# A two-layer graph attention kernel: index loads on two queues, another order of loads and products between the first heads, another split of the last tile

## Chip, cores and metric

One core of one Trainium2 chip. The metric is the device time of one execution in microseconds (us). Engines: TensorE (PE; its weight loads are listed as PEld), VectorE (DVE), ScalarE (ACT), GpSimd (POOL) and SyncE (SP, which only issues DMAs here). ScalarE and GpSimd issue DMAs too. A difference of 0.2% is 1.2 us.

## The reference

A graph of 512 nodes and 16,896 edges (8,192 pairs, each in both directions, and a loop at each node), sorted by destination. Two graph attention layers, a residual sum and a layer norm:

```python
def gat_layer(x, W, a_s, a_d, b, edge_index, concat):
    n = x.shape[0]
    H, C = a_s.shape
    h = (x @ W).reshape(n, H, C)
    src, dst = (edge_index[0], edge_index[1])
    alpha_s = jnp.einsum('nhc,hc->nh', h, a_s)
    alpha_d = jnp.einsum('nhc,hc->nh', h, a_d)
    e = jax.nn.leaky_relu(alpha_s[src] + alpha_d[dst], NEG_SLOPE)
    m = jax.ops.segment_max(e, dst, num_segments=n)
    e = jnp.exp(e - m[dst])
    denom = jax.ops.segment_sum(e, dst, num_segments=n)
    alpha = e / (denom[dst] + EPS)
    msg = h[src] * alpha[:, :, None]
    out = jax.ops.segment_sum(msg, dst, num_segments=n)
    ...
h = gat_layer(x, W1, a_src1, a_dst1, b1, edge_list, concat=True)   # 8 heads of 768
h = jax.nn.elu(h)
out = gat_layer(h, W2, a_src2, a_dst2, b2, edge_list, concat=True) # 1 head of 768
...
x = _layernorm(x + out, axis=-1)
```

x is 512 x 768, W1 768 x 6144, W2 6144 x 768, all float32.

## The kernel before

The edges are never gathered. A matrix `cnt` of 512 x 512 counts the edges of each pair of nodes, and the attention of a head is a dense 512 x 512 matrix: scores from two vectors of logits, a mask where the count is 0, an exponential, a row sum. All large products are float32, and are done by schemes that need fewer multiplications than the plain product: seven products instead of eight on halves (functions with `P1` to `P7`), or fifteen instead of eighteen on a 2 by 3 by 3 partition (`by_thirds`, `P0` to `P14`). Their sums of operands are made on VectorE or by DMAs that add into their target (`add_up`, issued by GpSimd), and each product that leaves PSUM is added to its place.

The order on every engine is the order in which the program is written (`manual_schedule`). The kernel is written out by hand in this order:

- **Start.** The edge indices are loaded as integers into `idx_i` (66 partitions; lines 94 to 96), then x and the weights of head 0 (lines 237 to 270). TensorE does matmuls of zeros meanwhile (`keep_warm`, lines 280 to 285). `idx_i` is cast to float32 (L372), turned by TensorE into `psi` (L376), and x's first chunks are turned (`turn_x`, L316, copied to `xT` by ScalarE, L317). VectorE makes `fold`, `low` and `rel` from `psi` (L382 to L387), from them the one-hot matrices (L739 to L761), and TensorE counts with them (L787) between the products of head 0's projection (L649, L431).
- **Heads 0 and 1.** The projection of head 1 (by halves), head 0's attended sum (`near_first`, L1078), head 0's share of the second layer (`second` by halves into `h2`, L1261 to L1311), and the projection of head 2 (L1408 to L1436, by halves, products P1, P2, P6, P7, P4, P5, P3 with two row blocks each; evictions at L470 to L476). In these stages the scores of the next head are made (`score`, `scored`), and each of its four tiles is weighed, scaled and parted: `turn_out` scales it on ScalarE (L967), parts the halves of its words (L970) and has SP issue a transposing DMA (L972); `turn_in` (L975) joins them again into `PT`.
- **Heads 1 to 6.** For each: the attended sum (`mixed`, L1038, three rounds of 28 matmuls of 128 x 256; it ends with the exponential linear unit, L984 to L987, which writes `gT`), then the head's share of the second layer (`second_by_thirds`: 15 products of 8 matmuls, L505), and the projection of the head after the next (15 products too).
- **End.** Head 7, the second layer's attention, and the result tile by tile (L1544 to L1575): product, residual, `bn_stats`, mean and deviation, scaling, store.

Lines that the prediction's steps touch. In `turn_out`, the two operations on ScalarE and the DMA:

```python
nc.scalar.activation(q, q, AF.Copy, scale=rden)                                    # L967
nc.scalar.copy(apart..., q...)                                                     # L970
nc.sync.dma_start(parted[t].rearrange("p (j d) -> p j d", d=P), apart, transpose=True)  # L972
```

In `by_thirds`, each product has an accumulation chain, a target and a sign. A chain keeps one PSUM bank; the bank is taken from the pool `mm` (5 banks) when the chain is first used:

```python
STEPS = dict(P8=("a", (1, 2), 1.0), P13=("x", (1, 2), -1.0), ..., P2=("y", (0, 0), 1.0), P4=("x", (1, 0), 1.0), ...
```

The left sides of head h's share (`g_thirds`): P2's is a part of `gT` as it is (chunks 0 and 3, first half of the nodes); P13's is made by VectorE from two parts (L1200). Products in `by_dma` are copied out by ScalarE (L515) and added into `h2` by a DMA that GpSimd issues (L516); others are added by VectorE (L518).

`load_a` (L220) loads a head's two attention vectors, each broadcast to 128 partitions, on SP's queue. `load_second` (L199) loads the second layer's weights of a head: `load_pairs`, `load_first` and `load_rest` issue loads on SP (L147, L153, L161) and additions on GpSimd (L135). The logits of head 2 are made at L1432 (`logits`, L449) behind the evictions of the products 10 and 12 of its projection.

Of the kernel before, what the change touches and what calls it, by code (L numbers as in the profile page):

```python
# [8 lines left out]
F32 = mybir.dt.float32  # L9
# [30 lines left out]
def gat_pass(  # L40
# [17 lines left out]
    P = 128  # L58
# [33 lines left out]


    idx_i = ohp.tile([EH, 2, 2, P], I32, name="idx_i")
    for j, v in enumerate((dst, src)):
        nc.sync.dma_start(idx_i[:, j], v.rearrange("(r c p) -> c r p", p=P, c=EH))

    def load_x():
        t_ = hpool.tile([P, NT, D], F32, name="hs")
# [120 lines left out]
    def load_a(h, a_s, a_d):  # L220
        A[h] = []
        for name, a in (("a_s", a_s), ("a_d", a_d)):
            v = wpool.tile([P, D], F32, name=name)
            nc.sync.dma_start(v, row_bcast(a))
            A[h].append(v)
# [9 lines left out]
        return m[r * HK * P:(r + 1) * HK * P, cols].rearrange("(k p) d -> p k d", p=P)  # L235

    w1_0 = w1[:, :D]
    for t in range(2):
        nc.scalar.dma_start(x_sb[:, t, L], x[t * P:(t + 1) * P, L])
    for k in range(HK):  # L240
        nc.sync.dma_start(W1[0][0][:, k, L], block(w1_0, 0, L)[:, k])
    for t in range(2):
# [37 lines left out]
    def keep_warm(n, cols=512):  # L280
        for _ in range(n):
            nc.tensor.matmul(idle[:, :cols], zeros[:, :P], zeros[:, :cols], start=True, stop=True)

    keep_warm(8, P)
    keep_warm(5)
    nodes = ohp.tile([P, N], F16, name="nodes")
    nc.gpsimd.iota(nodes, pattern=[[1, N]], base=0, channel_multiplier=0,
                   allow_small_or_imprecise_dtypes=True)
# [34 lines left out]
    if general:  # L323
        nc.vector.tensor_copy(idx_f, idx_i)
        idx = ohp.tile([P, 2, EC], F32, name="idx")
        psi = tr.tile([P, 512], F32, name="tr")
        for j in range(2):
            for r in range(2):
                nc.tensor.transpose(psi[:, (2 * j + r) * EH:(2 * j + r + 1) * EH], idx_f[:, j, r, :],
                                    ident[:EH, :EH])  # L330
        nc.vector.tensor_copy(idx, psi[:, :2 * EC].rearrange("p (j c) -> p j c", j=2))
    else:

        B = 32
        blocks = []
        for c in range(EC):
            m = (c + 0.5) * P * N / E
            b = int(m // B)  # L340
            slack = 2 + 16 * (m / N * (1 - m / N)) ** 0.5
            lo, hi = b - (m - b * B < slack), b + ((b + 1) * B - m < slack)
            blocks.append(range(max(lo, 0), min(hi, N // B - 1) + 1))
        assert max(map(len, blocks)) <= 2


        QC = EC // NT
        QW = QC + QC % 2
        base = ohp.tile([P, EC], F32, name="base")
        two = ohp.tile([P, NT, QW], F16, name="two")  # L350
        rel = ohp.tile([P, NT, QW], F16, name="rel")
        weight = ohp.tile([P, 3, NT, QW], BF16, name="weight")

        def fill(values, put):
            lo = 0
            while lo < EC:
                hi = lo + 1
                while hi < EC and values[hi] == values[lo] and hi % QC:
                    hi += 1
                put(lo, hi, float(values[lo]))  # L360
                lo = hi

        fill([b[0] * B for b in blocks], lambda lo, hi, v: nc.gpsimd.memset(base[:, lo:hi], v))
        fill([len(b) > 1 for b in blocks],
             lambda lo, hi, v: nc.gpsimd.memset(two[:, lo // QC, lo % QC:lo % QC + hi - lo], v))
        if QW > QC:
            nc.gpsimd.memset(rel[:, :, QC:], -1.0)
            nc.gpsimd.memset(two[:, :, QC:], 0.0)
            nc.gpsimd.memset(weight[:, :, :, QC:], 0.0)
        offsets = ohp.tile([P, B, QW], F16, name="offsets")  # L370
        nc.scalar.copy(offsets, nodes[:, :B].unsqueeze(2).to_broadcast([P, B, QW]))
        nc.vector.tensor_copy(idx_f, idx_i)  # L372
        psi = tr.tile([P, 512], F32, name="tr")
        for j in range(2):
            for r in range(2):
                nc.tensor.transpose(psi[:, j * EC + r * EH:j * EC + (r + 1) * EH], idx_f[:, j, r, :], ident[:EH, :EH])  # L376
        turn_x(0, 0)
        turn_x(1, 0)
        quarters = lambda v: v.rearrange("p (q c) -> p q c", c=QC)
        fold = ohp.tile([P, EC], F32, name="fold")  # L380
        low = ohp.tile([P, EC], F32, name="low")
        nc.vector.tensor_scalar(fold, psi[:, EC:2 * EC], float(HN), -float(HN), op0=ALU.is_ge, op1=ALU.mult)  # L382
        nc.vector.tensor_tensor(low, psi[:, EC:2 * EC], fold, op=ALU.add)
        nc.vector.tensor_tensor(rel[:, :, :QC], quarters(psi[:, :EC]), quarters(base), op=ALU.subtract)
        nc.gpsimd.tensor_scalar(weight[:, 2, :, :QC], quarters(fold), -(DIGIT - 1) / HN, 1.0, op0=ALU.mult, op1=ALU.add)
        nc.vector.scalar_tensor_tensor(two, rel, float(B), two, op0=ALU.is_ge, op1=ALU.mult)
        nc.vector.scalar_tensor_tensor(rel, two, -float(B), rel, op0=ALU.mult, op1=ALU.add)  # L387
        nc.gpsimd.tensor_tensor(weight[:, 1], weight[:, 2], two, op=ALU.mult)
        nc.gpsimd.tensor_tensor(weight[:, 0], weight[:, 2], weight[:, 1], op=ALU.subtract)
# [94 lines left out]

    def by_thirds(dest, A_, B_, order, fresh, by_dma=()):

        bank, begun, free = {}, set(), list(passed)

        def out(o):
            return dest[:, 2 * o[0]:2 * o[0] + 2, o[1] * TH:(o[1] + 1) * TH]  # L490

        def step(p):
            chain, o, sign = STEPS[p]
            copied = fresh and o not in begun
            begun.add(o)

            def multiply(between=None):
                first = chain not in bank
                if first:
                    bank[chain] = mm.tile([P, 512], F32, name="mm")  # L500
                for i in range(2):
                    for k in range(2):
                        if between and i == k == 1:
                            between()
                        nc.tensor.matmul(bank[chain][:, i * TH:(i + 1) * TH], A_[p][:, k, i * P:(i + 1) * P], B_[p][:, k, :],  # L505
                                         start=first and i == k == 0, stop=k == 1, skip_group_check=True)

            def empty():
                ps = bank[chain].rearrange("p (i n) -> p i n", i=2)
                if copied:  # L510
                    nc.scalar.activation(out(o), ps, AF.Copy, scale=sign)  # L511
                elif p in by_dma:
                    free.append(free.pop(0))
                    part = free[-1].rearrange("p (i n) -> p i n", i=2)
                    nc.scalar.activation(part, ps, AF.Copy, scale=sign)  # L515
                    nc.gpsimd.dma_start(out(o), part, accum_op=ALU.add)  # L516
                else:
                    nc.vector.tensor_tensor(out(o), out(o), ps, op=ALU.add if sign > 0 else ALU.subtract)  # L518
            return multiply, empty

        return [step(p) for p in order]
# [5 lines left out]
                         True)  # L527

    def second_by_thirds(h, A_, B_):
        return by_thirds(h2, A_, B_, ("P13", "P2", "P8", "P4", "P12", "P9", "P6", "P0", "P1", "P14", "P10", "P5", "P11", "P7", "P3"),  # L530
                         False, ("P13", "P2", "P8", "P0", "P7", "P3") if h + 2 < H else ("P13", "P2", "P8", "P0"))

    def second(A_, B_):
# [701 lines left out]
    def out_by_dma(t):  # L1235
        turn_out(q[t], t, weigh(q[t], t, scale=False))
# [4 lines left out]
    for h in range(H - 1):  # L1241
# [14 lines left out]
        if h == 0:  # L1256
# [26 lines left out]
            for n in range(2, 7):  # L1283
# [16 lines left out]
                if 3 < n < 6:  # L1300
                    out_by_dma(n - 4)
                if n == 6:
                    out_by_dma(3)
                    B2, sums2, load_pairs, load_first, load_rest = load_second(1)
                    load_pairs()
                    load_first()
                    load_rest()
                    load_a(2, a_src1[2], a_dst1[2])
                e1()
                if n < 5:  # L1310
                    fold_count(n - 1)  # L1311
# [94 lines left out]
        elif not last:  # L1406
            B_, sums = right(W1[h + 2], "w2")
            pairs = projection(h + 2, XA, B_)  # L1408
            for n in range(14):
# [6 lines left out]
                if n == 1:  # L1416
                    AA, sums3 = left_sums(h + 1)
                pairs[n][1]()
                if n in (1, 2, 4):
                    turn_in((n + 2) // 2)  # L1420
                if n == 5:
# [122 lines left out]
    for t in range(NT):  # L1544
# [21 lines left out]
        ours = slice(0, D)  # L1566
        if t + 1 == NT:

            ours = L
            off = small.tile([P, 1], F32, name="off")  # L1570
            nc.vector.scalar_tensor_tensor(off, mv[:, 0:1], -1.0, rstd, op0=ALU.mult, op1=ALU.mult)
            nc.scalar.activation(y[:, t, R], y[:, t, R], AF.Identity, bias=off, scale=rstd)
            nc.scalar.dma_start(out[t * P:(t + 1) * P, R], y[:, t, R])
        nc.vector.tensor_scalar(y[:, t, ours], y[:, t, ours], mv[:, 0:1], rstd, op0=ALU.subtract, op1=ALU.mult)
        nc.sync.dma_start(out[t * P:(t + 1) * P, ours], y[:, t, ours])  # L1575
    return again
# [29 lines left out]
```

## Time and profile before

| | us |
|---|---|
| median of 3 runs | 621.42 (621.12 to 622.11) |
| the profiled execution | 622.47 |
| its span, first to last instruction | 620.7 |

| engine | busy us | share of the span | instructions |
|---|---|---|---|
| PE | 610.5 | 98% | 2770 |
| PEld | 483.2 | 78% | 2770 |
| DVE | 522.7 | 84% | 1137 |
| ACT | 335.1 | 54% | 608 |
| POOL | 150.5 | 24% | 188 |

The span runs from the first to the last instruction of the profiled execution; 1.8 us of its time lie outside. Times of rows are counted from the span's start. A row of the timeline has start, length, engine, line, operation, output and inputs, shape and how many instructions are merged; a float32 matmul is listed as two. Matmuls overlap in the pipeline, so the distance between starts, and not the length, tells their pace.

### The profile page before, as it was taken

The numbers are of one execution on the slowest core, as the hardware profiler recorded it, in microseconds if no ns is written. First come the engines' busy times: TensorE is split into PE (matmuls) and PEld (weight loads), VectorE is DVE, ScalarE is ACT, GpSimd is POOL, SyncE is SP. The second block draws the span as 40 slices with busy tenths as digits, with TensorE's granted clock in tenths as the row PEclk, the third lists the DMA queues.
The fourth block names the chain that finished last, engine by engine and source line by source line (L and its number), as shares of the span: only waits on it lengthen the run. The fifth ranks groups of instructions, "written<-read, shape, count | busy, mean of one in ns | idle before, by whom it ended". The sixth has DMA issues, their size and how long they took to land.

```text
span 620.7 us, 8565 instructions
## 1 busy us (share of the span) xinstructions
PE 610.5 (98%) x2770; PEld 483.2 (78%) x2770; DVE 522.7 (84%) x1137; ACT 335.1 (54%) x608; POOL 150.5 (24%) x188
## 2 busy tenths in 40 slices
PE   8999999999999999999999999999999999999995
PEld 5655685556888888888888888888888888885553
DVE  5999979887899879977897878977897878978785
ACT  4766867721858056841858046751758046754361
POOL 2210011032352332413343333313342313010000
PEclk9999999999999999999999999999999999999998
DMA  8994777899999999999999999999999995690032
GB/s 283 319 248 79 202 184 248 165 280 300 219 219 192 277 258 219 162 301 233 220 216 204 273 255 227 160 273 248 226 218 199 304 283 90 129 286 10 17 77 80
DMA packets 109969, 130.05 MB, mean 210 GB/s; under 512 B 41638, under 2 KB 90846, under 8 KB 109150
## 3 DMA queue, kind: packets, MB, share of 16 engines
q1 hardware_dynamic: 75918, 91.94, 49.3%
q0 software_dynamic: 33568, 36.90, 38.7%
q10 hardware_dynamic: 432, 0.59, 0.3%
q8 instruction: 24, 0.39, 0.3%
q14 instruction: 27, 0.22, 0.1%
HBM read 100.43 MB, written 2.90 MB: 166 GB/s over the span
## 4 chain that ended last, share of the span: by engine, by line
PE 89%; DMA 4%; DVE 4%; ACT 1%; issue 0%; SPq 0%; DVEq 0%; ACTq 0%
PE mm L505 46%; PE mm L1038 18%; PE mm L431 11%; PE mm L1078 6%; PE mm L1552 3%; PE held L431 2%; DMA a_d<-in_L_gnn_a_dst_dram 2%; DMA w1r<-in_L_gnn_W_dram 1%; PE tr L787 1%; PE held L649 1%; DVE scr L440 1%; DMA zr<-pS 1%; DMA idx_i<-in_src_dram 1%; PE mm L316 0%; ACT pS L970 0%
## 5 line engine op out<-in xcount | busy, mean ns | idle before, releaser
L511 ACT ACTIVATE hs<-mm 128x512 f32<-128x512 f32 x30 | 17.9, 596 | 84.9 <-PE mm L505 84.4
L1038 PE MATMUL mm<-PT,hs 128*128 128x256 f32 x216 | 52.5, 379 | 0.0
L518 DVE TENSOR_TENSOR hs<-hs,mm 128x512 f32<-128x512 f32 x45 | 30.9, 686 | 22.2 <-PE mm L505 21.4
L690 ACT ACTIVATE q<-q,nmax 128x512 f32<-128x512 f32 x32 | 23.1, 721 | 49.0 <-DVE nmax L686 48.9
L516 POOL DMA_DIRECT2D h<-pass x22 | 26.5, 1319 | 80.9 <-ACT pass L515 80.9
L1038 PEld LDWEIGHTS mm<-PT,hs 128*128 128x128 f32 x216 | 41.0, 190 | 5.8
L518 DVE TENSOR_TENSOR h<-h,mm 128x512 f32<-128x512 f32 x56 | 38.3, 684 | 6.3 <-PE mm L505 5.7
L975 ACT COPY PT<-zr 128x1024 uint16<-128x1024 uint16 x34 | 39.3, 1157 | 4.8 <-DMA zr<-pS 3.5
L505 PE MATMUL mm<-w2r,xT 128*128 128x256 f32 x160 | 37.8, 379 | 0.0
L505 PE MATMUL mm<-w2r,gT 128*128 128x256 f32 x160 | 37.0, 379 | 0.0
L1038 PE MATMUL mm<-pS,gS 128*128 128x256 f32 x144 | 37.0, 379 | 0.0
L135 POOL DMA_DIRECT2D w1t<-in_L_gnn_W_dram x18 | 27.7, 1577 | 26.3 <-DVE hs L1002 20.9
L505 PE MATMUL mm<-w1t,hs 128*128 128x256 f32 x144 | 34.1, 380 | 0.0
L505 PE MATMUL mm<-w1r,hs 128*128 128x256 f32 x144 | 34.1, 379 | 0.0
L505 PE MATMUL mm<-w1r,gS 128*128 128x256 f32 x144 | 34.0, 379 | 0.0
L505 PEld LDWEIGHTS mm<-w2r,gT 128*128 128x128 f32 x160 | 30.4, 190 | 4.1
L505 PEld LDWEIGHTS mm<-w2r,xT 128*128 128x128 f32 x160 | 30.4, 190 | 4.1
L1042 ACT COPY u<-mm 128x256 f32<-128x256 f32 x18 | 6.7, 372 | 43.9 <-PE mm L1038 43.9
L505 PEld LDWEIGHTS mm<-w1t,hs 128*128 128x128 f32 x144 | 27.3, 190 | 3.9 <-ACT absent L515 0.2
L1038 PEld LDWEIGHTS mm<-pS,gS 128*128 128x128 f32 x144 | 27.4, 190 | 3.7
L505 PEld LDWEIGHTS mm<-w1r,hs 128*128 128x128 f32 x144 | 27.2, 190 | 3.8 <-DVE hs L1197 0.2
L505 PEld LDWEIGHTS mm<-w1r,gS 128*128 128x128 f32 x144 | 27.3, 190 | 3.7
(309 smaller groups left out, 1575.2 us busy)
## 6 DMA issues: line engine op xcount, KB each, us to landing
w2r<-in_L_gnn_W_dram SPq DMA_DIRECT2D x48, 384.0 KB
w1r<-in_L_gnn_W_dram SPq DMA_DIRECT2D x43, 384.0 KB
gT<-xd SPq DMA_DIRECT2D x5, 1280.0 KB
w1t<-in_L_gnn_W_dram SPq DMA_DIRECT2D x24, 256.0 KB
h<-pass POOLq DMA_DIRECT2D x22, 256.0 KB, 5.5
w1t<-in_L_gnn_W_dram POOLq DMA_DIRECT2D x18, 256.0 KB, 5.9
w2t<-in_L_gnn_W_dram SPq DMA_DIRECT2D x15, 256.0 KB
w2t<-in_L_gnn_W_dram POOLq DMA_DIRECT2D x15, 256.0 KB, 9.2
```

Source lines behind the costliest of these rows:

```text
L135: nc.gpsimd.dma_start(o, i, accum_op=ALU.add)
L431: nc.tensor.matmul(ps[:, :HALF], A_[p][:, k, i * P:(i + 1) * P], B_[p][:, k, :], start=start and k == 0, stop=k == HK - 1, skip_group_chec ...
L505: nc.tensor.matmul(bank[chain][:, i * TH:(i + 1) * TH], A_[p][:, k, i * P:(i + 1) * P], B_[p][:, k, :], start=first and i == k == 0, stop= ...
L511: nc.scalar.activation(out(o), ps, AF.Copy, scale=sign)
L516: nc.gpsimd.dma_start(out(o), part, accum_op=ALU.add)
L518: nc.vector.tensor_tensor(out(o), out(o), ps, op=ALU.add if sign > 0 else ALU.subtract)
L690: nc.scalar.activation(q, q, AF.Exp, bias=nmax, scale=-1.0, accum_out=dens[t])
L975: nc.scalar.copy(PT.rearrange("p s n -> p (s n)").bitcast(U16).rearrange("p (s n h) -> p s n h", s=NT, h=2)[:, :, t * P:(t + 1) * P, :], p ...
L1038: nc.tensor.matmul(bank[p][:, :HN], A_[p][:, k, c * P:(c + 1) * P], B_[p][:, k, :], start=over is None and k == 0, stop=k == 1, skip_group ...
L1042: nc.scalar.copy(u, part("P1"))
L1078: nc.tensor.matmul(banks[c, p][:, :HN], A_[p][:, k, c * P:(c + 1) * P], B_[p][:, k, :], start=over is None and k == 0, stop=k == 1, skip_g ...
L1552: nc.tensor.matmul(ps[:, :cols.stop - cols.start], PT[:, s, t * P:(t + 1) * P], h2[:, s, cols], start=(s == 2), stop=(s == 1))
```

## The change

Six edits.

1. The two index vectors are loaded by two queues (destinations by SP, sources by ScalarE), with 256 neighbouring indices in each partition instead of two pieces of 128. Of the two first tiles of x, the second goes from ScalarE's queue to SP's. The cast is done in two parts, sources on VectorE and destinations on ScalarE; each part is turned into a PSUM tile of its own, sources first.
2. Two more matmuls of zeros with 128 columns.
3. `second_by_thirds` begins with P2 and then P13. The bank of chain x is still taken before that of chain y.
4. Tile 3 of head 1's weights is weighed where it was, but scaled and parted behind the first copy out of PSUM of head 2's projection.
5. The attention vectors of head 2 are loaded before head 1's weights of the second layer, and both behind tile 3's transposing DMA.
6. In the last tile, VectorE scales 512 columns and ScalarE 256 (384 each before); each part is stored by its own DMA.

```diff
-    for j, v in enumerate((dst, src)):
-        nc.sync.dma_start(idx_i[:, j], v.rearrange("(r c p) -> c r p", p=P, c=EH))
+    for j, (queue, v) in enumerate(((nc.sync, dst), (nc.scalar, src))):
+        queue.dma_start(idx_i[:, j], v.rearrange("(c r p) -> c r p", p=P, r=2))
...
-    for t in range(2):
-        nc.scalar.dma_start(x_sb[:, t, L], x[t * P:(t + 1) * P, L])
+    for t, queue in enumerate((nc.scalar, nc.sync)):
+        queue.dma_start(x_sb[:, t, L], x[t * P:(t + 1) * P, L])
...
     keep_warm(8, P)
     keep_warm(5)
+    keep_warm(2, P)
...
-        nc.vector.tensor_copy(idx_f, idx_i)
-        psi = tr.tile([P, 512], F32, name="tr")
-        for j in range(2):
+        nc.vector.tensor_copy(idx_f[:, 1], idx_i[:, 1])
+        nc.scalar.copy(idx_f[:, 0], idx_i[:, 0])
+        psi = {}
+        for j in (1, 0):
+            psi[j] = tr.tile([P, 512], F32, name="tr")[:, :EC]
             for r in range(2):
-                nc.tensor.transpose(psi[:, j * EC + r * EH:j * EC + (r + 1) * EH], idx_f[:, j, r, :], ident[:EH, :EH])
+                nc.tensor.transpose(psi[j].rearrange("p (c r) -> p r c", r=2)[:, r, :], idx_f[:, j, r, :], ident[:EH, :EH])
...
     def by_thirds(dest, A_, B_, order, fresh, by_dma=()):
-        bank, begun, free = {}, set(), list(passed)
+        bank, begun, grown, free = {}, set(), set(), list(passed)
...
-                first = chain not in bank
-                if first:
-                    bank[chain] = mm.tile([P, 512], F32, name="mm")
+                first = chain not in grown
+                grown.add(chain)
+                for c in (chain,) if fresh else ("x", chain):
+                    if c not in bank:
+                        bank[c] = mm.tile([P, 512], F32, name="mm")
...
     def second_by_thirds(h, A_, B_):
-        return by_thirds(h2, A_, B_, ("P13", "P2", "P8", "P4", ...
+        return by_thirds(h2, A_, B_, ("P2", "P13", "P8", "P4", ...
...
                 if n == 6:
-                    out_by_dma(3)
-                    B2, sums2, load_pairs, load_first, load_rest = load_second(1)
-                    load_pairs()
-                    load_first()
-                    load_rest()
-                    load_a(2, a_src1[2], a_dst1[2])
+                    rden3 = weigh(q[3], 3, scale=False)
                 e1()
...
                 pairs[n][1]()
+                if n == 0:
+                    turn_out(q[3], 3, rden3)
+                    load_a(2, a_src1[2], a_dst1[2])
+                    B2, sums2, load_pairs, load_first, load_rest = load_second(1)
+                    load_pairs()
+                    load_first()
+                    load_rest()
...
-            ours = L
+            ours = slice(0, HALF + P)
+            theirs = slice(HALF + P, D)
...
-            nc.scalar.activation(y[:, t, R], y[:, t, R], AF.Identity, bias=off, scale=rstd)
-            nc.scalar.dma_start(out[t * P:(t + 1) * P, R], y[:, t, R])
+            nc.scalar.activation(y[:, t, theirs], y[:, t, theirs], AF.Identity, bias=off, scale=rstd)
+            nc.scalar.dma_start(out[t * P:(t + 1) * P, theirs], y[:, t, theirs])
```

## The prediction

> **What bounds the kernel now.** I read the page first. Sections 1 and 2: TensorE is busy 98% of the span, and only the first and the last slices are not full. So a gain can come only from gaps in TensorE's row and from the two ends.
>
> ```profile
> span 620.7 us, 8565 instructions
> PE   8999999999999999999999999999999999999995
> ```
>
> The waits of TensorE (PE, its matmuls, and PEld, its weight loads) name the gaps; the columns are total us, times, longest.
>
> ```profile
> PE tr L376 <- DVE idx_f L372: 0.9, 1, 0.9
> PE mm L431 <- DVE hs L475: 0.8, 1, 0.8
> PE mm L431 <- ACT hs L470: 0.3, 1, 0.3
> PEld mm L505 <- DVE absent L1200: 1.6, 6, 0.3
> ```
>
> The chain that ended last tells what stood before each of them (start, length, what):
>
> ```profile
> 1.33 3.17 DMA idx_i<-in_src_dram
> 4.60 0.43 DVE idx_f L372
> 5.17 0.67 PE tr L376 x4
> ...
> 122.00 1.05 ACT nr L970
> 123.05 0.39 ACT hs L470
> ...
> 132.28 11.94 DMA a_d<-in_L_gnn_a_dst_dram
> 144.21 0.03 issue
> 144.24 0.02 DVEq L449
> 144.26 0.04 issue
> 144.30 0.97 DVE scr L449 x2
> 145.27 0.48 DVE hs L475
> ```
>
> The timeline gives the size of each gap by the distance between starts. TensorE, at the start and at the first product by thirds:
>
> ```profile
> 5.63 1.49 PE L316 MATMUL mm<-ident,hs 128*128 128x128 f32 x6
> 7.05 3.72 PE L649 MATMUL held<-w1r,xT 128*128 128x384 f32 x8
> 10.60 0.82 PE L316 MATMUL mm<-ident,hs 128*128 128x128 f32 x6
> ```
> ```profile
> 165.10 1.10 PE L1038 MATMUL mm<-PT,gS 128*128 128x256 f32 x4
> 166.13 1.99 PE L505 MATMUL mm<-w1t,absent 128*128 128x256 f32 x8
> 167.96 1.89 PE L505 MATMUL mm<-w1t,gT 128*128 128x256 f32 x8
> ```
>
> The first block shows a second thing: six transposes take 1.49 us at 5.63 and 0.82 us at 10.60. TensorE runs at about half its rate until some 8.8 us; there the starts of single matmuls go from 0.64 us apart to 0.32.
>
> The profiled execution took 622.47 us: span 620.7 and 1.8 around it. The median is 621.42. The changes below are read from the span and taken off the median, with the 1.8 left as it is.
>
> **The fourth tile parted behind a copy.** Twelve matmuls of 128x384 start 3.87 us apart (127.45, 131.32, 135.19). From 119.16 the next twelve should start at 123.03, and the twelve after them at 126.90; they start at 123.47 and 127.45. Loss 0.55. The cause is ScalarE's order: scale and parting copy of tile 3 (0.72 and 1.05) stand before the first copy out of PSUM (L470), which ends at 123.42. After the change that copy follows tile 2's parting copy, which ends at 121.34, so it ends near 121.8, 1.2 before the matmul needs it. The second L470 copy now stands behind tile 3's two operations: 121.8 + 0.72 + 1.05 + 0.48 = 124.0; its reader, the next product, comes at 124.97. Cover 0.9; past it each us costs one. SP's transposing DMA starts some 0.5 later; its reader turn_in(3) ran at 128.02, and the sum that uses it (L1011) at 132.06. Nothing there. Gain 0.55.
>
> **Attention vectors ahead of W2.** a_s and a_d of head 2 are issued at 130.71 and 132.28, behind ten W2 loads, and a_d lands at 144.2. The logits (L449) wait on VectorE, and queued behind them is the eviction L475 that frees the bank for the last three matmuls. TensorE's row 142.93 x6 should be followed at 146.80 by the next stage; that starts at 147.84. Loss 1.04. Issued before W2, the vectors have some 18 us to land, where the longest landing here was 11.94. Without the wait VectorE does L475 (to 141.75), two logits (1.92) and L475 again by 144.2, on the old times; the matmul needs it at 144.86. Gain 1.04. Price: SP issues two loads first (0.86 + 0.34) and starts 0.5 later, so W2 comes up to 1.7 later. Its first reader on VectorE is L172 at 161.34, its first product is at 166. The last sum that L172 needs (the add into P14) is issued by POOL at 134.78, and such adds land in 5.9 at the median: 141, or 143 with the delay. Cover 18 us.
>
> **Raw product first.** Per stage, 4 + 8 matmuls at 0.216 need 2.59; from 165.10 to 167.96 it is 2.86 (loss 0.27), and in the five later stages 2.71 (235.35 to 238.06; loss 0.12). TensorE waits for L1200, which makes P13's left side. P2's left side is gT itself, chunks 0 and 3, written far earlier; P13 then starts 1.73 later, when L1200 has long ended. ScalarE copies P2 out first and P13 second, half a us later; P13's bank is wanted by P4, which stood 1.25 behind that copy in head 1. In head 6 a score operation (0.71) lies between the two copies and the margin is about nil, so I count 0.05 there. Gain 0.27 + 4 x 0.12 + 0.05 = 0.80. On POOL, P13's add into h2 is issued one DMA later (up to 1.2); P8's add, which waits for it, and the two pair adds behind it move by as much. Their reader (L172, 198.88) is 10 us behind (182.69 + 5.9).
>
> **The start.** The source indices were SP's second load (issue 1.33, landed 4.50); as ScalarE's first they issue at 0.82, so land near 4.0. Half the cast (0.42 for all; about 0.25) ends near 4.35 and the transposes start near 4.5 instead of 5.17. The warm matmuls end at 4.25, or 4.46 with two more of 0.11; they stay in front and cost nothing; if the indices came sooner, up to 0.2. The other half is cast on ScalarE, idle from 4.12 to 6.52 (some 0.37, as a 128x256 copy): second pair near 4.65. Gain 0.68 for all that follows, if x has landed half a us sooner than it was used; no view shows its landing. x changes places with indices on both queues at nearly the same issue times (1.2 to 1.3).
>
> What the 0.68 is worth hangs on the clock. Eight held matmuls need 7 x 0.3225 + 0.49 = 2.75 and took 3.72: 0.97 lost; the six transposes lost 0.67. TensorE's first run (1.08 to 4.25, 3.17 us) didn't lift the rate; after a gap of 0.92, it rose 3.7 into the second run. With the gap closed the run counts from 1.08, and the same 3.7 puts the rise near 5: then most of 0.97 and part of the 0.67 come on top, 0.68 + 0.97 + 0.3 = 1.95 at most. If the rise stays at 8.8, half of the earlier start is spent at half rate: 0.34. VectorE begins 0.9 earlier (first transposes are those that fold needs) and has an idle 1.32 at 13.4 that a faster TensorE fills, but its sum L564 needs a weight load whose landing no view shows. I take 1.4, near the upper end. The Trainium skill (TensorE: Matmul & The Clock Gate, the section Part 1: The HAM clock gate) says that the clock is released after a busy window of about 3.4 us, and that these windows run freely, whatever the kernel does. This trace agrees as far as it goes: 3.17 us of work left the rate low. By that rule the rise comes 0 to 3.4 us after the first full window has begun, so it would differ from run to run; the gain by it is still between the two ends above.
>
> **The end.** The last chain is ScalarE's half (L1572, 0.71, DMA issue at 616.06). At 256 columns I take 0.5 (a 128x256 activation from SBUF: 0.49), so the issue is at 615.86. VectorE's 512 columns lie between 0.47 for 384 and 0.68 for 768: 0.54, issue 615.77 instead of 615.70. The same 384 KB go out, so I count 0.1 of the 0.2; ends +0.3 and -0.2, the latter if SP's larger piece lands last.
>
> **Sum.** 0.55 + 1.04 + 0.80 + 1.4 + 0.1 = 3.89. 621.42 - 3.89 = 617.5.
>
> **The rivals.** (A) The clock rises no earlier: start 0.34, sum 2.83, 618.6. For it: the rise depends on the whole gap being closed; a late x would leave one. Chance 0.25. (B) The start's gain is given back before 120: VectorE has no idle time from 34 to 65, and its chain runs from 92 to 112. Left are 0.55 + 1.04 + 0.80 + 0.1: 618.9. Against it: VectorE starts earlier too. 0.12. (C) W1's right halves or x land late enough that nothing but the two middle gaps goes (1.59): 619.8. 0.08. (D) Slower: the first product's bank is not free. In each of six stages P2 uses the second bank taken after the mixed stage. If that is the bank which L1059 still reads (to 167.68), P2 starts at 167.73 instead of 165.96: 1.77 lost where 0.27 or 0.12 was, so +1.5 + 5 x 1.65 = 9.8, less the other gains of 3.1: 628. It decides from a release later than 165.9, and makes the whole slower once 0.65 a stage is lost. In the old order P2 came after that time, so its start doesn't exclude it. Against it: five banks, and the two freed longest ago were left at 160.54 (head 1's second round) and 162.96 (L1046). 0.04.
>
> **How the numbers follow.** Forecast 0.50, A 0.25, B 0.12, C 0.08, D 0.04, 0.01 for the rest. The likeliest is 617.5. Low end: start 1.95 and end 0.3 give 616.7, less some tenths of scatter: 616.5. High end: A, B and half of C: 619.5. About 0.2% (1.2 us) can be told from no change here. Forecast, A, B and C are all beyond it: 0.91 faster with a little off for combined shortfalls, 0.05 within, 0.04 slower.
>
> **What would show it.** Right: no wait of L376 on a cast; the held matmuls 0.32 apart from the first; no wait on L470 or L475; the row after 142 unbroken; P2's eight matmuls 0.86 behind the last four of the mixed stage; last issue by ScalarE 0.2 sooner after its rstd. Wrong: a wait of P2 on ScalarE or VectorE six times, held matmuls still 0.64 apart, or new waits on W2 near 161.

## The result and the profile after

The changed kernel took 618.76 us (median of 8 runs, 618.36 to 620.97), the kernel before 622.24 beside it (8 runs, 621.12 to 623.52): ratio 0.995, 95% interval 0.9935 to 0.9966. A second measurement of the same two kernels gave 619.04 (12 runs) and 621.96 (27 runs): ratio 0.9962 (0.9948 to 0.9975). By the medians the change takes off 2.9 to 3.5 us, by the ratios, which weigh all runs, 2.4 to 3.1; 3.9 were forecast, and 617.5.

The profiled execution took 618.36, of which the span is 616.5. The page, sections 1 and 2: the first slice of TensorE is now full.

```profile
span 616.5 us, 8568 instructions
PE   9999999999999999999999999999999999999995
```

The waits of TensorE (total us, times, longest): of the four shown of before, none is left, the six for L1200 included. On the matmuls' own rows there remain the start of the zeros and one new short wait, for the copy of `xT`.

```profile
PE bc L282 <- DVE zeros L276: 1.1, 1, 1.1
PE held L654 <- ACT xT L318: 0.2, 1, 0.2
```

TensorE's timeline, at the start, in head 2's projection and at the first product by thirds (lines are 1 to 8 higher than before):

```profile
4.27 0.85 PE L379 MATMUL tr<-ident,idx_f 66*128 66x66 f32 x4
4.91 1.02 PE L317 MATMUL mm<-ident,hs 128*128 128x128 f32 x6
6.17 2.85 PE L654 MATMUL held<-w1r,xT 128*128 128x384 f32 x8 [0.24 <-ACT xT L318]
8.85 0.82 PE L317 MATMUL mm<-ident,hs 128*128 128x128 f32 x6
...
117.52 7.90 PE L434 MATMUL mm<-w2r,xT 128*128 128x384 f32 x24
...
140.74 4.03 PE L434 MATMUL mm<-w2r,xS 128*128 128x384 f32 x12
144.61 1.03 PE L1043 MATMUL mm<-PT,hs 128*128 128x256 f32 x4
...
161.88 1.10 PE L1043 MATMUL mm<-PT,gS 128*128 128x256 f32 x4
162.82 1.89 PE L510 MATMUL mm<-w1t,gT 128*128 128x256 f32 x8
```

The index transposes start at 4.27 (5.17 before), the held matmuls are at full rate from the first (2.85 for eight, 3.72 before), the 24 matmuls from 117.52 run through, and so do the twelve from 140.74. P2 follows the mixed stage's last four after 0.94.

Where the time went is read from the distance of the same milestone in both traces, after against before:

| start of | before | after | gained so far |
|---|---|---|---|
| first P2 of head 0's projection | 12.55 | 10.80 | 1.75 |
| head 0's share of the second layer | 92.04 | 90.39 | 1.65 |
| mixed sum of head 1 | 147.84 | 144.61 | 3.23 |
| mixed sum of head 2 | 218.09 | 214.63 | 3.46 |
| head 7's attended sum | 543.37 | 539.45 | 3.92 |
| last matmul | 613.31 | 609.40 | 3.91 |
| end of the span | 620.67 | 616.48 | 4.19 |

### The profile page after: what moved, and what is told of

Its sections match the earlier page's. It is cut to its first block, busy times and chain, and to the rows that moved or that the text cites. A ratio compares the mean times of both kernels' runs of the same rounds, so it can differ in the third digit from the quotient of the medians.

```text
span 616.5 us, 8568 instructions
## 1 busy us (share of the span) xinstructions
PE 608.3 (99%) x2772; PEld 483.1 (78%) x2772; DVE 523.5 (85%) x1137; ACT 335.5 (54%) x609; POOL 150.8 (24%) x188
## 4 chain that ended last, share of the span: by engine, by line
PE 98%; DVE 0%; ACT 0%; issue 0%; DVEq 0%
PE mm L510 46%; PE mm L434 20%; PE mm L1043 18%; PE mm L1083 6%; PE mm L1559 3%; PE held L434 2%; PE tr L792 1%; PE held L654 1%; PE bc L282 1%; PE mm L317 0%; PE bc L792 0%; PE tr L1468 0%; PE tr L964 0%; PE bc L1503 0%; DVE hs L1563 0%; PE tr L1505 0%
## 5 line engine op out<-in xcount | busy, mean ns | idle before, releaser
L980 ACT COPY PT<-zr 128x1024 uint16<-128x1024 uint16 x34 | 39.3, 1157 | 5.5 <-DMA zr<-pS 3.0
L135 POOL DMA_DIRECT2D w1t<-in_L_gnn_W_dram x18 | 29.0, 1843 | 26.7 <-DVE xS L1147 26.1
```

What stands on the lines that cost most here:

```text
L135: nc.gpsimd.dma_start(o, i, accum_op=ALU.add)
L980: nc.scalar.copy(PT.rearrange("p s n -> p (s n)").bitcast(U16).rearrange("p (s n h) -> p s n h", s=NT, h=2)[:, :, t * P:(t + 1) * P, :], p ...
```

## Experiments on the start

Two things changed at once at the start: the indices come sooner, and the clock rises sooner. In the trace's record of the granted clock full rate begins at 8.84 in the kernel before and at 5.30 in the changed one; "the rise" is this time from here on, and "P2" in this section is the first P2 of head 0's projection. Four kernels try to part the two.

**The gap closed with zeros, the indices left late.** The kernel before, and:

```diff
     keep_warm(5)
+    keep_warm(9, P)
```

> The kernel before with nine more matmuls of zeros (128 columns) behind the warm ones, so that TensorE has no gap from 4.25 to 5.17; nothing else is changed, the indices land as late as before. Clock theory (an unbroken run from 1.08 lifts the rate near 5, as it does at 5.3 in the changed kernel): the held matmuls start 0.32 apart from the first, 0.97 less there and some 0.3 to 0.4 less in the transposes; span 619.3 to 619.8 instead of 620.7, median about 1.2 below the kernel before. Issue theory (the start's gain is the indices' earlier landing, and the rate's rise is chance): no difference, 0 to 0.2 slower.

620.86 (12 runs) against 622.20: ratio 0.9992 (0.9978 to 1.0006), not to be told from no change. In its profile the rise was at 5.54 and head 0's P2 at 11.54, 1.01 sooner than in the kernel before. The zeros did not close the gap whole: the cast began at 5.00 here, 4.60 in the kernel before, and TensorE still waited for it.

```profile
PE tr L377 <- DVE idx_f L373: 0.4, 1, 0.4
```

The span of 618.5 is 2.2 below the one shown of before, while the medians differ by 1.3 and the means by 0.7: a first sign that one profile of each is not the pair of kernels. So the profile is as the clock theory has it, and the runs decide between the two theories only weakly.

**The indices early, the clock late.** The changed kernel without the two zeros; and with still fewer (`keep_warm(3)` in place of `keep_warm(5)`, and no two):

```diff
     keep_warm(5)
-    keep_warm(2, P)
```

> The changed kernel without its two extra matmuls of zeros. Clock theory: the first transposes are ready near 4.27, the warm matmuls end at 4.25, so the run is hardly broken: span 616.3 to 616.8, as the changed kernel. If the two are what keeps the run whole: a gap of some tenths, the rise a window later, span 617.5 to 618.

> The changed kernel with three warm matmuls of 512 columns instead of five and none of the two small ones, so that TensorE idles from about 3.4 to the first transposes near 4.3: the indices land early, but the run is broken by about 0.9 as in the kernel before. Clock theory: the rise comes a window later (near 8.7), held matmuls 0.64 apart, 1.0 to 1.4 longer than the changed kernel, span 617.5 to 618. Issue theory: span 616.5.

619.86 (0.9965, 0.995 to 0.9979) and 620.24 (0.9976, 0.9963 to 0.9988). The rise came at 10.45 and 10.01, and the held matmuls show it; TensorE's timeline of the first of the two:

```profile
4.26 0.86 PE L378 MATMUL tr<-ident,idx_f 66*128 66x66 f32 x4
4.91 1.49 PE L316 MATMUL mm<-ident,hs 128*128 128x128 f32 x6
6.33 4.87 PE L653 MATMUL held<-w1r,xT 128*128 128x384 f32 x8
```

The transposes start as early as in the changed kernel, but eight held matmuls take 4.87 instead of 2.85, and P2 starts at 12.98 and 12.76, later than in the kernel before. With the rise 1.2 to 1.6 later than in the first profile of before, the early indices don't show in P2 at all. This holds for these two profiles. The runs of the first of the two kernels spread from 617.84 to 622.20, its profiled one took 621.00, and its ratio of 0.9965 can't be told from the 0.9962 of the changed kernel: what the two zeros of edit 2 are worth is not shown.

**The start alone.** The kernel before with edits 1 and 2.

> The kernel before with edits 1 and 2 alone (indices on two queues, two casts, two more matmuls of zeros). If the parts add up: 1.75 less, the distance at which the two traces stand from 14 to 74 us; of this 0.09 given back at the first attended sum: span 619.0. If the rest of the kernel swallows it (VectorE's chain from 92 to 112 and ScalarE's up to 123.5): span 620 to 620.7, and the stall at 123.47 grows by what was gained.

620.59 (12 runs): 0.9984 (0.9971 to 0.9996). Rise 6.96, P2 at 11.26, 1.29 sooner, and 1.28 of it was left at the last matmul: in this profile what the start gains isn't given back later, as rival B had supposed it would be.

**Both kernels a second time.**

> The changed kernel as it is, a second time, for the scatter of its start. Theory (the clock rises at the end of the first whole interval of 3.41 us that is busy, and the intervals' phase differs from run to run): the first matmul of zeros is at 1.08, so the rise lies between 4.5 and 7.9, and the first P2 of head 0 starts at 10.80 + 0.5 x (rise - 5.30), so between 10.4 and 12.1; everything behind it as in the first profile, the last matmul 598.6 behind that P2 to within 0.2. Median 618.4 to 619.4, runs spread over 2 us. Rival (the rise depends on this kernel's work alone): the rise is again within 0.1 of 5.30, P2 at 10.80, span 616.5, and the runs differ for another reason.

> The kernel before as it is, a second profile. Theory: the rise is anywhere between 5.4 and 12, P2 of head 0 starts at 12.55 + 0.5 x (rise - 8.84); the wait for the logits behind a_d's landing is again between 0.2 and 1.0 us, the wait for the first copy 0 to 0.3, the six waits of P13's left side again 1.6 in all. Median 621.5 to 622.5. Rival: rise within 0.1 of 8.84 and P2 within 0.1 of 12.55.

The times stand above and in the next lines; the profiles matter more. The changed kernel's rise was at 6.92, P2 at 11.23 (I expected 11.6, so half a us for each us of rise is too much between 5 and 7). The kernel before had its rise at 4.41 this time, not 8.84 (I expected 5.4 to 12; for 4.41 the line of the expectation puts P2 at 10.3, and it was at 11.05), and with it half-rate matmuls were gone behind the zeros although TensorE still waited for the cast. Its timeline:

```profile
1.07 3.17 PE L282 MATMUL bc<-zeros 128*128 128x128 bf16 x13 [1.07 <-DVE zeros L276]
5.08 0.44 PE L376 MATMUL tr<-ident,idx_f 66*128 66x66 f32 x4 [0.84 <-DVE idx_f L372]
5.36 0.82 PE L316 MATMUL mm<-ident,hs 128*128 128x128 f32 x6
6.42 2.85 PE L649 MATMUL held<-w1r,xT 128*128 128x384 f32 x8 [0.24 <-ACT xT L317]
```

That execution took 620.23, and the kernel's twelve runs fall apart into four of 620.23 to 620.58, one of 621.18 and seven of 621.86 to 622.80. One program, and two starts in its two profiles; that the two groups of runs are these two starts is likely, but not shown. Sorted by rise, P2 of head 0 starts:

| | rise early | rise late |
|---|---|---|
| indices late | 11.05 (4.41), 11.54 (5.54) | 12.55 (8.84) |
| indices early | 10.80 (5.30), 11.23 (6.92), 11.26 (6.96) | 12.76 (10.01), 12.98 (10.45) |

Between rises of 6.96 and 10.01 the early indices' P2 would lie at 12.2 for 8.84; against 12.55 they are worth about 0.4 there; at 5.54 the line from 10.80 to 11.23 gives 10.86 against 11.54, some 0.7. These figures are rough: the profiles of the sections below, also with early indices, lie up to 0.3 off such a line (10.51 at 4.53, 10.96 at 5.84, 11.22 at 5.86, 11.14 at 6.74), and of the 0.7 some 0.4 is the late cast of the gap-closed profile. The rest of the profiled 1.75, over 1 us, is the clock, and in another run of the kernel before that part was there without the change.

**The wait of 0.24 filled.** The changed kernel with two more zeros ahead of the held matmuls:

```diff
         turn_x(1, 0)
+        keep_warm(2, P)
```

> The changed kernel with two more matmuls of zeros (128 columns) between the transposes of x and the first held matmuls, where TensorE waited 0.24 us for the copy of xT. Theory: the wait is filled, P2's start stays on the line 10.80 + 0.5 x (rise - 5.30) within 0.15, and since the changed kernel's intervals are busy enough already, median and spread are those of its second run beside it, within 0.5 us. Rival: in some runs of the changed kernel an interval misses by that wait and the rise comes 3.4 us later; then the filled one loses its slowest runs and its median is 0.3 to 0.8 lower.

618.60 (10 runs) against 619.04 for the changed kernel beside it: ratio to before 0.9953 (0.9938 to 0.9969) against 0.9962 (0.9948 to 0.9975). The theory said the same within 0.5, and 0.44 isn't to be told from that. The rise was at 3.96, sooner than the 4.5 I had given as its earliest, and P2 at 10.70, where the line of the expectation puts 10.13: the line doesn't hold for so early a rise. For the rival speaks that one of its 10 runs lies above 620, and 3 of 12 of the changed kernel's; it stays open.

## Experiments on the middle

**Tile 3 ahead of the copy again** (edit 4 undone):

```diff
-                    rden3 = weigh(q[3], 3, scale=False)
+                    out_by_dma(3)
...
-                    turn_out(q[3], 3, rden3)
```

> The changed kernel with edit 4 undone: tile 3 is scaled and parted before the first copy out of PSUM. Theory (ScalarE's order made the stall): the third group of six matmuls of head 2's projection starts 0.44 late again and the two row blocks take 0.55 more, from the projection's first matmul to the mixed stage 27.64 instead of 27.09. Rival (the vectors' landing, or SP's order, made it): no stall. The start of the clock's full rate differs from run to run, so the stage is read, not the span.

619.34 (10 runs): 0.9967 (0.9948 to 0.9985), in the runs not to be told from the changed kernel. In its profile head 2's projection lost 0.23, not 0.55: the first 24 matmuls, which need 7.74, took 7.97 to the next row.

```profile
117.90 8.13 PE L434 MATMUL mm<-w2r,xT 128*128 128x384 f32 x24
125.87 4.03 PE L434 MATMUL mm<-w2t,xS 128*128 128x384 f32 x12
```

The copy L473 stood behind tile 3's two operations as before, but all of ScalarE's row was sooner, because a copy ahead of them (`turn_in`, L980 here, L975 in the kernel before) had nothing to wait for. ScalarE's timeline of the kernel before has that wait:

```profile
118.48 1.16 ACT L975 COPY PT<-zr 128x1024 uint16<-128x1024 uint16 x1 [0.23 <-DMA zr<-pS]
```

In the start-alone kernel the same copy waited 0.27, and TensorE lost some 0.6. In the second profile of the kernel before it didn't wait, and there TensorE lost 0.23: 24 matmuls from 117.68, the next row at 125.65, which is 7.97 where 7.74 are needed. So the stall was 0.2 to 0.6, by the landing of one transposing DMA. With the edit it was 0 in either case: in the profile of the even split (below) the copy waited 0.26 and the projection lost nothing.

**The vectors behind W2 again** (edit 5 undone, both still behind tile 3's DMA):

```diff
-                    load_a(2, a_src1[2], a_dst1[2])
                     B2, sums2, load_pairs, load_first, load_rest = load_second(1)
                     load_pairs()
                     load_first()
                     load_rest()
+                    load_a(2, a_src1[2], a_dst1[2])
```

> The changed kernel with edit 5 undone: a_s and a_d of head 2 are loaded behind head 1's W2 again. Theory: the logits wait, and the last three matmuls of the projection start late by 0.2 to 1.0 (0.7 to 1.0 in two kernels with the old order so far, 0.2 in a third, so the landing varies). Rival (the stall came from the W2 loads' own place, which stays late here): no stall.

621.96 (10 runs): 0.9998 (0.9983 to 1.0013). In the changed kernel this order of loads costs about all that the other five edits gain. TensorE's and VectorE's timelines:

```profile
140.35 2.10 PE L434 MATMUL mm<-w2r,xS 128*128 128x384 f32 x6
144.37 3.89 PE L434 MATMUL mm<-w2r,xS 128*128 128x384 f32 x6 [1.92 <-DVE hs L478]
148.10 1.03 PE L1043 MATMUL mm<-PT,hs 128*128 128x256 f32 x4
```
```profile
141.01 0.96 DVE L452 SCALAR_TENSOR_TENSOR scr<-hs,a_s 128x768 bf16<-128x768 f32 x1 [1.84 <-DMA a_s<-in_L_gnn_a_src_dram]
142.88 0.96 DVE L452 SCALAR_TENSOR_TENSOR scr<-hs,a_d 128x768 bf16<-128x768 f32 x1 [0.90 <-DMA a_d<-in_L_gnn_a_dst_dram]
143.76 0.55 DVE L478 TENSOR_TENSOR hs<-mm,hs 128x384 f32<-128x384 f32 x1
```

The mechanism is the one forecast: logits wait for a load, the eviction waits behind them, TensorE waits for the bank. The price has two parts. The wait itself is 1.92. The second part no one had in the sum: six matmuls that need 1.94 took 3.73 to the next row, at half rate. The table by stretches (us, busy us of PE, PEld, DVE, ACT and POOL, then PEclk, the granted clock) shows it:

```profile
141.06:144.47 3.41, 1.49 (x6) 0.61 (x4) 2.51 (x6) 0.00 (x0) 0.23 (x1) 1.00 1.03 345
144.47:147.89 3.42, 3.42 (x6) 1.90 (x7) 2.15 (x5) 0.00 (x0) 0.26 (x1) 0.50 1.10 181
147.89:151.30 3.41, 3.41 (x16) 2.92 (x16) 1.99 (x5) 0.37 (x1) 0.93 (x1) 1.00 0.61 118
```

A stretch of 3.41 us with TensorE busy 1.49 was followed by one at 0.50. Head 2's projection took 3.88 more than in the changed kernel (30.97 against 27.09). I had expected 0.2 to 1.0. The half-rate stretch seems not to have come in every run: three of the ten, the profiled one among them, have a mean granted clock of 0.994, the others 0.996 to 0.999. The wait, too, is longer than the 0.77 of the kernel before, by 1.15: counted from the start of the projection, the logits of the second vector began at 25.75 here and at 25.14 there, and TensorE comes to them 0.55 sooner, because the stall that edit 4 removes is gone. So the two middle gaps are not independent: closing the first alone makes the second longer.

**P13 first again** (edit 3 undone):

```diff
-        ... ("P2", "P13", "P8", "P4", ...
+        ... ("P13", "P2", "P8", "P4", ...
```

> The changed kernel with P13 first again. Theory: 0.23 more in head 1's stage, 0.11 more in each of heads 2 to 5, nothing in head 6 (there the gain of the order was taken back by another wait): 0.67 between the first mixed stage and the last attended sum. Rival (the shorter stages come from the earlier start of the stage and not from the order): no difference.

618.91 (4 runs): 0.9947 (0.9927 to 0.9966), too few runs to place 0.7 us in the median. The profile does: the wait is back, six times,

```profile
PEld mm L510 <- DVE absent L1205: 1.6, 6, 0.3
```

and from the mixed sum of head 1 to head 7's attended sum it is 0.70 longer than the changed kernel: 0.24 in head 1, 0.11 to 0.12 in heads 2 to 5, nothing in head 6.

**Head 5 alone in the old order** (on the filled kernel). In the second profile of the changed kernel TensorE waited at 482.97, in the projection behind head 5, and that stage took 70.40, which is 0.47 more than in the first profile and 0.36 more than in the kernel before. Its lines, TensorE, ScalarE and GpSimd:

```profile
480.85 1.89 PE L510 MATMUL mm<-w2r,xT 128*128 128x256 f32 x8
482.97 1.97 PE L510 MATMUL mm<-w2r,gT 128*128 128x256 f32 x8 [0.23 <-DVE pS L1017]
```
```profile
477.57 1.16 ACT L980 COPY PT<-zr 128x1024 uint16<-128x1024 uint16 x1 [1.10 <-DMA zr<-nr]
```
```profile
478.96 1.19 POOL L135 DMA_DIRECT2D w2t<-in_L_gnn_W_dram  x1 [7.91 <-DVE w2r L172]
```

The names in the brackets aren't the last to come. In the first profile L1017 ended at 482.55 and the same matmul had started at 482.26, so it isn't that. What moves together is ScalarE's copy (its end 478.73 here, 477.92 there), GpSimd's add 0.23 behind that end, and TensorE's weight load 3.98 behind the add's issue.

```diff
+        first_ = ("P13", "P2") if h == 5 else ("P2", "P13")
```

> The filled kernel (two more matmuls of zeros ahead of the first held ones) with P13 first again in head 5 alone. Theory: raw product first has a price that was not seen: GpSimd's add of P13 and all that is queued behind it come 2.3 us later (458.95 against 456.55 reckoned from the same row of TensorE), SP's last transposing DMA of that head lands later, ScalarE's copy L980 waits for it 0.6 to 1.1 us, GpSimd's add into w2t is issued 0.8 to 1.1 us behind that copy's start and its reader on TensorE starts 4.0 later, up to 0.36 late. With the old order in head 5 the wait of L980 there is gone, TensorE has no wait on L1017, and the stage from the mixed sum of head 5 to that of head 6 takes 70.04 us as before (it took 69.93 without and 70.40 with the wait). Against the filled kernel: +0.12 where that had no wait, -0.2 where it had; median within 0.4 of it. Rival: the wait comes from the DMA queues alone; then it is there at head 5 with the old order too, 0.3 us or more.

618.93 (7 runs): 0.9953 (0.9936 to 0.997). In head 5 all came as the theory says: no wait of the copy, none of TensorE, and the stage was as long as before. Over the fourteen profiles, that copy in head 5 waited 0.27 to 1.10 in all eight with P2 first there, and not at all in the six with P13 first. GpSimd's third add of that stage, P8's, is issued 34.0 to 34.7 behind the start of head 5's mixed sum with P2 first, and 31.8 to 33.1 behind it with P13 first: on the mean 2.1 later. (P13's own add, which the expectation names, comes only 0.7 later.) How a later add makes a later transposing DMA, these runs do not show. And the loss went elsewhere: head 4, still with P2 first, lost 0.62 against the kernel before instead of gaining 0.11, by two waits of ScalarE of 1.49 for such DMAs and this line of TensorE:

```profile
407.39 3.72 PE L511 MATMUL mm<-w2t,xS 128*128 128x256 f32 x16 [0.47 <-ACT hs L517]
```

So nothing was won by it, and no version tried can be told from the changed kernel as better.

Over all fourteen profiles, TensorE loses 0.25 to 0.73 in one head's stage (2, 4 or 5) in five of the nine with P2 first (one of them in all heads but 5), and in none of the five that have P13 first in every head. That is 0.26 on the mean of the nine, off the 0.70 that the order gains. ScalarE's copy waits for such DMAs in the old order too, up to 2.0, but there no wait reached TensorE.

## The experiment on the end

**384 to 384 again** (edit 6 undone):

```diff
-            ours = slice(0, HALF + P)
-            theirs = slice(HALF + P, D)
+            ours = slice(0, HALF)
+            theirs = slice(HALF, D)
```

> The changed kernel with 384 and 384 columns in the last tile. Theory: ScalarE's operation takes 0.71 instead of 0.60, its DMA is issued 0.11 later, and the end comes 0.1 to 0.3 later after the last matmul: 7.8 to 8.0 instead of 7.70. Rival (the same bytes on the same 16 engines): no difference beyond 0.05.

618.70 (5 runs): 0.9955 (0.9933 to 0.9976). ScalarE's part with its issue, in the changed kernel:

```profile
611.42 0.60 ACT L1580 ACTIVATE hs<-hs,off,rstd 128x256 f32<-128x256 f32 x1 [0.43 <-DVE off L1579]
611.87 0.33 SPq L1583 DMA_DIRECT2D out_dram<-hs  x1
612.05 0.36 ACTq L1581 DMA_DIRECT2D out_dram<-hs  x1
```

and with even halves:

```profile
611.74 0.71 ACT L1580 ACTIVATE hs<-hs,off,rstd 128x384 f32<-128x384 f32 x1 [0.42 <-DVE off L1579]
612.12 0.33 SPq L1583 DMA_DIRECT2D out_dram<-hs  x1
612.47 0.36 ACTq L1581 DMA_DIRECT2D out_dram<-hs  x1
```

From the activation's start to the last issue it is 0.63 against 0.73: 0.10 sooner. From the last matmul to the end of the span it is 7.08 against 7.06, so the rival's "no difference" came and not the 0.1 to 0.3 that I had expected. Over the profiles this tail lies between 7.05 and 7.45 whatever the split, which is more than the 0.10.

## Why the prediction was right, and where it was off

The direction and the size class held: 618.76 lies within 616.5 to 619.5 and faster by 3.5. It lies 1.3 above the forecast, nearer to rival A's 618.6 and B's 618.9, though neither mechanism was seen in its two profiles. Of the 1.3, 0.8 is the base: the forecast took 3.9 off 621.42, the median of three runs, and the eight runs of the kernel before beside the result have 622.24. What was over-counted is 0.4 of the 3.9 by the first pair of medians and 1.0 by the second.

- **The two middle gaps, 0.55 + 1.04 = 1.59.** In the profiled pair 1.58 went (3.23 less 1.65). Right for that trace, too large for the kernel: the gaps hang on landings. From head 2's projection to the mixed sum the first profile of the kernel before loses 1.59, the start-alone kernel 1.58, the second profile of before 0.82 and the gap-closed one 0.72. In the eight profiles with edits 4 and 5 none of it is left; on the four without, the mean is 1.17. The step that failed is the reading of one execution as the kernel's price. W2's delay cost nothing, as argued.
- **Raw product first, 0.80.** 0.70 measured; head 6 gave 0, where 0.05 was counted. The price named for GpSimd, "up to 1.2" later with a reader 10 us behind, was wrong twice: P8's add came 2.1 later on the mean, and in another chain (transposing DMA, ScalarE's copy, add into w2t) no slack was left. Where this order stood, TensorE lost 0 and 0.47 against the expected pace in the two profiles of the changed kernel, and 0.73 in head 4 of the last experiment; that the order is the cause is shown for head 5 by the last experiment, and for the other heads only by the count of profiles.
- **The start, 1.4 between 0.34 and 1.95.** 1.75 in the profiled pair, from a rise of 8.84 against 5.30. The transposes came 0.90 sooner where 0.68 were counted: the sources' cast took 0.86 and not 0.25, but began at 3.26, where the prediction has it begin near 4.1. The step "the same 3.7 puts the rise near 5" was no law of the gap: the rise was seen at 5.30 and 6.92 in the changed kernel, at 8.84 and 4.41 in the one before. Rival A's premise, that the rise hangs on the whole gap, fell the same way: before's second profile had the whole gap and an early rise. Nor does the prediction's "0 to 3.4 us after the first full window has begun" follow from the rule that it quotes: a full window first takes its own 3.4 us. The start-alone runs, 0.16% under before with an interval of 0.04% to 0.29%, agree with about 1 us on the mean. Of the 1.75, 0.10 went in head 0's attended sum, in some profiles and not in others; B's full loss wasn't seen.
- **The end, 0.1.** The issue came 0.10 sooner instead of 0.2, since the activation took 0.60 and not 0.5. On the span it gave nothing that shows; the 0.28 that the table has behind the last matmul is within the scatter of that tail.
- **Rival D (P2's bank not free).** P2 started 0.94 behind the last four matmuls (0.86 forecast) and then went on; TensorE had no wait there in any of the six stages.

The profiled pair gained 4.19 in span and 4.11 in time, more than the medians' 2.9 to 3.5, because that execution of before had a late rise and late landings, and that of after an early rise. By the means that the runs bear out, 1.17 + (0.70 - 0.26) + about 1 + 0 is an estimate of 2.6 for the change, within the 2.4 to 3.1 of the ratios.

## What to carry to other kernels

A gap that ends on a DMA's landing is worth its mean over several executions, and one trace gives a single draw: take a second profile before counting tenths. Where a load is moved past others on its queue, ask who is queued behind its reader; here two small loads behind ten large ones cost about as much as the whole change gained. And an edit that pushes a queue back can cost as scatter, a loss in some executions and none in others, so follow that queue, GpSimd's here, to all of its readers.

## What the runs showed of the clock

- In every profile, each stretch of one granted clock in the record, from the first rise on and up to the last fall, is a whole number of 3.413 us (607.57 is 178 of them), and the phase differs from run to run: rises lay between 3.96 and 10.45. The Trainium skill (TensorE: Matmul & The Clock Gate, Part 1: The HAM clock gate) says that the window is 3413 ns and runs freely; the record agrees.
- How much idle time such a window bears is bounded roughly. By the distances between starts TensorE was idle for some 0.44 in the start-alone kernel's window (3.55 to 6.96), 0.52 in the filled one's (0.55 to 3.96, the zeros beginning at 1.07) and 0.54 in the gap-closed one's (2.12 to 5.54), and the rate rose after each. With some 0.66 (no two zeros, 3.62 to 7.04) and 1.1 (kernel before, 2.02 to 5.43) it stayed low. These are estimates: the rows' own ends, which are modelled, leave only 0.02 idle in the window without the two zeros.
- Once up, the rate fell after one window with 1.92 of 3.41 idle, for one window. It stayed up after 1.81 (filled kernel, 608.12 to 611.54, behind its last matmul) and after 0.92 (second profile of before, 4.41 to 7.82). The same page of the Trainium skill, in its section HAM oscillation, gives as the abstract rule no idle gaps of over about 3.4 us; here the measurement decides, and 1.92 was enough.
